# Where the sums stand between the scores: a graph attention kernel with one round behind every second set, its own places in a block's first group, and edges loaded in four parts

## The chip, the cores and the metric

The kernel runs on one core of one Trainium2 chip. The metric is the device time of one execution in microseconds (us); lower is better. Three runs of the kernel before gave 10911.48, 10919.42 and 10927.48 us, median 10919.42.

## What is computed

Four graph layers act on `x` (3327 nodes, 128 features) with one adjacency matrix `adj` (3327 x 3327). Each ends in a residual addition and a layer norm. The change touches only layer 0, an attention in which the edges are added twice to the scores:

```python
q = (x @ Wq.T).reshape(d, n, h)      # d = 128, n = 3327, h = 8
k = (x @ Wk.T).reshape(d, n, h)
v = (x @ Wv.T).reshape(d, n, h)
a = jnp.einsum('dnh,dmh->dnm', q, k) * d ** -0.5
a = a + adj + adj
a = jax.nn.softmax(a, axis=2)
out = jnp.einsum('dnm,dmh->dnh', a, v).reshape(n, h * d) @ Wo.T
x = layernorm(x + out)
```

So there are 128 attention matrices of 3327 x 3327, each with only 8 values to a row of q, k and v: 1.4 thousand million exponentials, for which the scores are a cheap product and the sums another one.

## The kernel before, in words

**Blocks, steps, sets.** The queries are cut into seven chunks of 476 columns (`CW`), the keys into four stretches of 7, 7, 6 and 6 tiles of 128 (`KBS`). A chunk with a stretch is a block; there are 28, half of them seven-tile, half six-tile. In a block the kernel goes through the 128 steps `d`. Within a step the tiles form three sets: of 3, 2 and 2 tiles in a seven-tile block, of 2, 2 and 2 in a six-tile block (`SETS`, L444). Each set has its own region of PSUM, three regions in all (`sc`, L421), and one more bank, `o`, takes the sums.

**Scores.** The edges of a block are loaded into one tile `e_in` (L429 to L441) and, at step 0, turned into PSUM by transposes (L603). They then stay there for all 128 steps. Each step adds the difference of its scores to those of the step before (L610, 64 rows: the query and key halves of this step and, negated, of the step before), so the region always holds edges plus this step's scores. The exponential of a set (L618, on ScalarE) reads the region; the scores of the next step may only be added once it has ended.

**VectorE's share.** In some groups of four steps (`on_vector`, L446) the third set of the first step is not given to ScalarE: `vector_exp` (L568) computes its exponential on VectorE in nine passes, of which only the first (L574) reads PSUM. In a seven-tile block these are the groups g with g mod 4 = 0, 1, 2, in a six-tile block the even g.

**Sums.** Four steps form a group; a block has 32 groups. While the scores of one group are made, the sums of the group before are: `weigh` (L624) multiplies one key tile of the four steps with the padded values, four matmuls of 32 columns each side by side (L635, two instructions each). I call this a round. A group needs seven or six rounds. `PLACES` (L452) says behind which of the twelve sets of the group (place 0 to 11, three to a step) how many rounds stand; a number that occurs twice means two rounds in a row. The pattern is chosen by the number of tiles of the block that the rounds belong to and by g mod 4. After every third group (and the last) the sums in `o` are added to `acc` by VectorE (`flush`, L642 to L650); the first round of the next group starts `o` anew and has to wait for that.

**Order.** TensorE, ScalarE, GpSimd and VectorE run in the order in which the loop at L670 to L682 records their instructions. `prepare` (L546), at the first step of each group, issues on the SP queue the queries and keys two groups ahead (`load_heads`, L456; 1.25 MB in a seven-tile block: `kt` and `qt`, three buffers each) and the values one group ahead. GpSimd then copies the values into a padded tile (L515). VectorE copies the queries of the next group within its partitions (L499 to L501), asked for at step 0 of a group with a VectorE set and at step 1 of the others. VectorE's passes wait in a list and are recorded in small portions by a running account of costs (`clock`, L585).

**Background.** Beside the attention the kernel transposes `adj` in 91 pieces of 512 x 256, one per eight groups (`PACE`). `background` (L526), at groups n with n mod 8 = 0, stores the piece that is done (sixteen DMAs on the GpSimd queue, L234) and loads the next one (L184; a piece at the edge of the matrix first has a memset on GpSimd, L176 or L178). `background_work` transposes it on VectorE at n mod 8 = 3 and takes its sums at 7. `ai`, `at` and `e_in` have one buffer each. The edges of the next block are asked for at step 0, behind the last set (L621): two DMAs on the SP queue, of 1344 KB and the rest.

**After the attention** come the output product and layers 1 to 3, from about 10150 us on, with TensorE as the busiest engine.

Of the kernel before, what the change touches and what calls it, by code (L numbers as in the profile page):

```python
# [10 lines left out]
F32 = mybir.dt.float32  # L11
# [8 lines left out]
P = 128  # L20
GROUP = 4
# [3 lines left out]
PACE = 8  # L25
CW = 476
# [24 lines left out]
def kernel(ctx: ExitStack, tc: tile.TileContext, x, adj, wq, wk, wv, wo,  # L51
# [14 lines left out]
    nc = tc.nc  # L66
    N, D = x.shape
# [26 lines left out]
    def flat_ap(dram, at, pattern):  # L94

        f = dram.rearrange("r c -> (r c)")
        if isinstance(at, int):
            base = f[at:at + 1]
        else:
            base = f[ds(at, 1)]  # L100
        return bass.AP(base.tensor, base.offset, pattern)
# [143 lines left out]
    with tc.tile_pool(name="pw", bufs=1) as pw, tc.tile_pool(name="pa", bufs=2) as pa, \  # L245
# [12 lines left out]
        for u in range(NU):  # L258
# [4 lines left out]
            for a, n in ([(0, P)] if full == P else [(0, 112), (112, full - 112)]):  # L263
                nc.sync.dma_start(out=xr[a:a + n, 0:R, :],
                                  in_=flat_ap(x, (base + R * a) * D, [[R * D, n], [1, R * D]]))
            if rest:
                nc.sync.dma_start(out=xr[full:full + 1, 0:rest, :],
                                  in_=flat_ap(x, (base + R * full) * D, [[D, 1], [1, rest * D]]))
# [87 lines left out]
        d = 0  # L356
# [52 lines left out]
    def attention():  # L409
        with tc.tile_pool(name="acc", bufs=1) as accp, tc.tile_pool(name="kq", bufs=3) as kq, \  # L410
# [12 lines left out]
            subs = [(j, min(P, CW - j)) for j in range(0, CW, P)]  # L423
# [2 lines left out]
            groups = [(b, g) for b in range(len(blocks)) for g in range(NHG)]  # L426
            steps = [(b, d) for b in range(len(blocks)) for d in range(D)]

            def load_edges(b):  # L429
                c0, kb = blocks[b]  # L430
                k0, nt = KBS[kb]
                w = min(nt * P, N - k0 * P)
                e = ed.tile([P, len(subs), 7 * P], F32, name="e_in")
                if w < nt * P:
                    nc.gpsimd.memset(e[:, :, w:nt * P], 0.0)
                nf = CW // P
                nc.sync.dma_start(out=e[:, 0:nf, 0:w],
                                  in_=flat_ap(adj, c0 * N + k0 * P, [[N, P], [P * N, nf], [1, w]]))
                nc.sync.dma_start(out=e[0:CW - nf * P, nf, 0:w],
                                  in_=flat_ap(adj, c0 * N + (nf * P * N + k0 * P), [[N, CW - nf * P], [1, w]]))  # L440
                return e  # L441


            SETS = {7: [(0, 3), (3, 2), (5, 2)], 6: [(0, 2), (2, 2), (4, 2)]}  # L444

            def on_vector(nt, g):  # L446

                return g % 4 != 3 if nt == 7 else g % 2 == 0

            PLACES = {7: ((0, 0, 4, 7, 7, 10, 10), (0, 0, 4, 7, 7, 9, 10), (1, 1, 4, 6, 8, 10, 10),  # L452
                          (0, 2, 3, 5, 7, 8, 10)),
                      6: ((0, 0, 3, 6, 8, 10), (0, 2, 4, 5, 7, 9)) * 2}

            def load_heads(b, g):  # L456

# [66 lines left out]
            loaded, worked, turning = [], [], []  # L524

            def background(n):  # L526
                if n % PACE == 0 and worked:
                    piece_store(pe, *worked.pop(0))
                if n % PACE == 0 and pieces:
                    u, c = pieces.pop(0)  # L530
                    loaded.append((u, c, piece_load(pe, u, c)))

            def background_work(n):
                if n % PACE == 3 and loaded:
                    u, c, ai = loaded.pop(0)
                    steps = piece_work(pe, u, c, ai)
                    worked.append((u, c, next(steps)))
                    next(steps)
                    clock[1] += 2.4
                    turning.append(steps)  # L540
                if n % PACE == 7 and turning:
                    clock[1] += 2.4
                    for _ in turning.pop():
                        pass
# [49 lines left out]
            def exponents(b, d, si):  # L594
                kb = blocks[b][1]
                nt = KBS[kb][1]
                t0, n = SETS[nt][si]
                s = sc[si]
                if d == 0:
                    for i in range(n):  # L600
                        tl = tile_at(nt, t0 + i)[2]
                        for j, (q0, w) in enumerate(subs):
                            nc.tensor.matmul(s[:, i, q0:q0 + w], lhsT=edges[b][0:w, j, tl * P:(tl + 1) * P],  # L603
                                             rhs=ident[0:w, 0:w], is_transpose=True,
                                             start=(j == 0), stop=True, skip_group_check=True)
                kt, qt = heads[b, d // GROUP]
                k = d % GROUP
                for i in range(n):
                    rg, pos, _ = tile_at(nt, t0 + i)
                    nc.tensor.matmul(s[:, i, 0:CW], lhsT=kt[64 * rg:64 * rg + 64, k, pos * P:(pos + 1) * P],  # L610
                                     rhs=qt[64 * rg:64 * rg + 64, k, :],
                                     start=False, stop=True, skip_group_check=True)
                e = ex.tile([P, (3, 2, 2)[si], CW], F32, tag=f"e{si}", name=f"e{si}", bufs=(6, 7, 8)[si])
                if on_vector(nt, d // GROUP) and (d % GROUP, si) == (0, 2):
                    vector_exp(e[:, 0:n, :], s[:, 0:n, 0:CW], (b, d // GROUP))
                    clock[1] += 1.2
                else:
                    nc.scalar.activation(e[:, 0:n, :], s[:, 0:n, 0:CW], AF.Exp, scale=2.0)  # L618
                for i in range(n):
                    es[b, d, t0 + i] = e[:, i, :]  # L620
                if d == 0 and si == len(SETS[nt]) - 1 and b + 1 < len(blocks):  # L621
                    edges[b + 1] = load_edges(b + 1)

            def weigh(b, g, r):  # L624

# [35 lines left out]
            queue, place = [], 0  # L661
            with tc.manual_schedule(engines={mybir.EngineType.PE, mybir.EngineType.Activation,
                                             mybir.EngineType.Pool, mybir.EngineType.DVE}):
                edges[0] = load_edges(0)
                for n in range(2):
                    heads[groups[n]] = load_heads(*groups[n])
                for _, _, step in copy_queries(*groups[0]):
                    step()
                values[groups[0]] = load_values(*groups[0])
                for b, d in steps:  # L670
                    prepare(b, d)
                    for si in range(len(SETS[KBS[blocks[b][1]][1]])):
                        vector_work(b)
                        exponents(b, d, si)
                        for _ in range(PLACES[len(queue_of)][d // GROUP % 4].count(place) if queue else 0):
                            weigh(*queue.pop(0))
                        place += 1
                    if d % GROUP == GROUP - 1:
                        while queue:
                            weigh(*queue.pop(0))  # L680
                        queue_of = [(b, d // GROUP, r) for r in range(KBS[blocks[b][1]][1])]
                        queue, place = list(queue_of), 0  # L682
                while queue:
                    weigh(*queue.pop(0))
                while stores:
                    store(*stores.pop(0))
# [558 lines left out]
```

## Time and profile before

| | |
|---|---|
| median of three runs | 10919.42 us |
| the profiled execution's own time | 10915.5 us |
| its span, first to last instruction | 10913.7 us |
| granted TensorE clock, mean | 0.995 |
| TensorE matmuls, weight loads busy | 97%, 38% of the span |
| ScalarE busy | 90% |
| VectorE busy | 77% |
| GpSimd busy | 15% |
| first exponential starts, last one ends | 334.9, 10141.6 us |
| ScalarE busy in the first and second seven-tile block shown below | 362.43 and 362.32 us |
| the six-tile blocks after them | 319.66 and 319.87 us |

How to read it: a group line names line, engine, operation, tiles, shapes and count, then busy time and mean duration, then the idle time of the engine just before these instructions and what ended it. A timeline line names start, duration, engine, line, operation and count of merged instructions, with the idle time before the first in brackets. "PEld" is TensorE's loading of weights, "SPq" the queue in which SyncE issues DMAs. Matmuls are pipelined and their ends are modelled, so 97% does not say that TensorE has nothing to give. The stretches of four blocks, 1739.8 to 3137.4 us, with busy time and count of each engine, the clock and the share of the DMA engines:

```profile
1739.80:2110.00 370.20, 363.27 (x2712) 128.56 (x2708) 326.48 (x344) 362.43 (x360) 68.86 (x108) 1.00 0.86 129
2110.00:2479.30 369.30, 363.00 (x2715) 128.46 (x2711) 325.97 (x344) 362.32 (x361) 60.75 (x98) 1.00 0.84 126
2479.30:2808.00 328.70, 320.76 (x2340) 106.83 (x2336) 251.35 (x276) 319.66 (x369) 58.00 (x103) 1.00 0.83 129
2808.00:3137.40 329.40, 321.10 (x2337) 107.12 (x2333) 250.33 (x272) 319.87 (x370) 74.07 (x132) 1.00 0.86 135
```

The columns after the stretch are its length, then TensorE's matmuls, its weight loads, VectorE, ScalarE and GpSimd.

### The profile page before, as it was taken

How to read it: one execution, taken by the hardware profiler on the slowest of the kernel's cores; microseconds unless marked ns; L12 is line 12 of the kernel's file. 1: busy time of each engine (PE TensorE's matmuls, PEld its weight loads, DVE VectorE, ACT ScalarE, POOL GpSimd, SP SyncE). 2: the span in 40 equal slices, each digit the busy share in tenths (PEclk: the TensorE clock that was granted, in tenths of full speed). 3: DMA queues.
4: the chain of work that ended last, by engine and by line, in shares of the span. 5: the costliest groups of instructions: out<-in, count | busy, mean ns of one | idle time of the engine just before them, and what ended most of it. 6: DMA issues, size and time to landing. Idle time of an engine off the chain costs nothing. (4 is left out here: it accounts for less than half of the span.)

```text
span 10913.7 us, 202710 instructions
## 1 busy us (share of the span) xinstructions
PE 10590.0 (97%) x76941; PEld 4114.5 (38%) x76941; DVE 8351.7 (77%) x9359; ACT 9774.0 (90%) x10671; POOL 1667.9 (15%) x2742
## 2 busy tenths in 40 slices
PE   8899999999999999999999999999999999999999
PEld 5333333333333333333333333333333333333779
DVE  6788778887788877788877888778887788777312
ACT  3799999999999999999999999999999999999400
POOL 0111122111221111211112111121111100001200
PEclk9899999999999999999999999999999999999999
DMA  7888888888888888888888888888888888788676
GB/s 252 155 127 123 129 133 133 128 124 127 136 133 128 124 127 131 136 123 127 131 131 135 115 122 121 123 133 129 126 129 123 120 119 117 116 111 118 209 283 245
DMA packets 995063, 1516.19 MB, mean 139 GB/s; under 512 B 202471, under 2 KB 812577, under 8 KB 980267
## 3 DMA queue, kind: packets, MB, share of 16 engines
q1 hardware_dynamic: 896854, 1371.75, 77.5%
q0 software_dynamic: 79616, 116.88, 4.7%
q8 instruction: 623, 10.21, 0.5%
q10 hardware_dynamic: 17620, 14.49, 0.4%
q14 instruction: 350, 2.87, 0.1%
HBM read 1371.86 MB, written 130.35 MB: 138 GB/s over the span
## 5 line engine op out<-in xcount | busy, mean ns | idle before, releaser
L618 ACT ACTIVATE e<-sc 128x952 f32<-128x952 f32 (+1 forms) x10192 | 9551.3, 1076 | 281.1 <-PE sc L610 274.7
L635 PE MATMUL o<-e,v_pad 128*32 128x476 f32 (+1 forms) x46592 | 5657.5, 573 | 47.1 <-DVE acc L648 39.8
L610 PE MATMUL sc<-qt,kt 64*128 64x476 f32 x23296 | 4503.2, 439 | 178.4 <-ACT e L618 113.1
L610 PEld LDWEIGHTS sc<-qt,kt 64*128 64x128 f32 x23296 | 2197.0, 184 | 4570.9 <-ACT e L618 4015.0
L580 DVE SCALAR_TENSOR_TENSOR e<-e,ey 128x952 f32<-128x952 f32 x1680 | 1932.7, 1150 | 52.3
L515 POOL COPY v_pad<-vs 128x192 f32<-128x192 f32 (+1 forms) x896 | 534.4, 622 | 7986.1 <-DMA vs<-v_img 5559.1
L635 PEld LDWEIGHTS o<-e,v_pad 128*32 128x32 f32 (+1 forms) x46592 | 1027.9, 108 | 1904.7 <-issue 1858.7
L574 DVE TENSOR_SCALAR ey<-sc 128x952 f32<-128x952 f32 x560 | 643.9, 1150 | 1047.2 <-PE sc L610 1041.2
L501 DVE CAST qt<-qt 64x1904 fp32r<-64x1904 f32 x896 | 1032.8, 1153 | 30.4
L499 DVE TENSOR_SCALAR qt<-qt 32x1428 fp32r<-32x1428 f32 x896 | 807.6, 901 | 159.2 <-DMA qt<-q_s 100.6
L234 POOL DMA_DIRECT2D adjT_s<-at x1352 | 785.3, 587 | 234.5 <-DMA adjT_s<-at 162.2
L580 DVE SCALAR_TENSOR_TENSOR e<-e,et 128x952 f32<-128x952 f32 x560 | 647.5, 1156 | 17.8
L576 DVE SCALAR_TENSOR_TENSOR ey<-et,ey 128x952 f32<-128x952 f32 x560 | 645.1, 1152 | 19.4
L580 DVE SCALAR_TENSOR_TENSOR e<-ey 128x952 f32<-128x952 f32 x560 | 642.0, 1146 | 0.0
L1081 PE MATMUL bank<-y,eT 128*128 128x128 f32 (+1 forms) x4056 | 473.9, 276 | 0.4 <-DVE h L1203 0.4
L1081 PEld LDWEIGHTS bank<-y,eT 128*128 128x128 f32 (+1 forms) x4056 | 465.3, 192 | 5.7 <-DVE h L1203 0.6
L648 DVE TENSOR_TENSOR acc<-o,acc 128x476 f32<-128x476 f32 x231 | 150.3, 651 | 312.4 <-PE o L635 312.0
L575 DVE TENSOR_SCALAR et<-ey 128x952 f32<-128x952 f32 x560 | 372.6, 665 | 18.7
L577 DVE TENSOR_SCALAR et<-et 128x952 int32<-128x952 int32 x560 | 371.1, 663 | 19.3
L500 DVE TENSOR_SCALAR qt<-qt 32x476 fp32r<-32x476 f32 x896 | 360.2, 402 | 7.8 <-DMA qt<-lead_s 3.5
L1041 ACT ACTIVATE rstd<-mv,eps 128x1 f32<-128x1 f32 x104 | 30.4, 293 | 265.5 <-DVE mv L1039 265.5
L655 POOL DMA_DIRECT2D o_s<-acc x308 | 191.4, 625 | 34.9 <-DVE acc L648 22.0
(152 smaller groups left out, 2402.6 us busy)
## 6 DMA issues: line engine op xcount, KB each, us to landing
kt<-k_s SPq DMA_DIRECT2D x5320, 96.0 KB
kt<-k_s SPq DMA_DIRECT2D x1764, 128.0 KB
eT<-adjT_s SPq DMA_DIRECT2D x78, 1664.0 KB
qt<-q_s SPq DMA_DIRECT2D x896, 119.0 KB
qt<-q_s SPq DMA_DIRECT2D x1792, 59.5 KB
vs<-v_img SPq DMA_DIRECT2D x224, 224.0 KB
adjT_s<-at POOLq DMA_DIRECT2D x1352, 32.0 KB, 6.0
vs<-v_img SPq DMA_DIRECT2D x224, 192.0 KB
```

What stands on the lines that cost most here:

```text
L234: nc.gpsimd.dma_start(out=flat_ap(adjT_s, (t * P + 32 * q) * NP + c * PIECE, [[NP, 32], [P, ns], [1, P]]), in_=at[32 * i:32 * i + 32].rear ...
L499: return [(0.9, None, lambda: nc.vector.tensor_scalar(qt[32:64, 1:], qf[0:32, 0:GROUP - 1], -1.0, None, ALU.mult)), (0.4, None, lambda: nc ...
L501: (1.2, None, lambda: nc.vector.tensor_copy(qt[64:128], qf[0:64]))]
L515: nc.gpsimd.tensor_copy(vp[:, 32:32 + nt * GROUP * 32].rearrange("p (x c) -> p x c", c=32)[:, :, 0:H], vs.rearrange("p (x c) -> p x c", c=H))
L574: nc.vector.tensor_scalar(y, x, -58 * math.log(2.0), 2 / math.log(2.0), ALU.max, ALU.mult)
L575: vec.append((0.7, of, lambda: nc.vector.tensor_scalar(t, y, ROUND, None, ALU.add)))
L576: vec.append((1.2, of, lambda: nc.vector.scalar_tensor_tensor(y, t, ROUND, y, ALU.subtract, ALU.subtract)))
L580: vec.append((1.2, of, lambda i=i, a=a: nc.vector.scalar_tensor_tensor(e, e if i else y, a, t if i == len(POLY) - 1 else y, ALU.add, ALU.m ...
L610: nc.tensor.matmul(s[:, i, 0:CW], lhsT=kt[64 * rg:64 * rg + 64, k, pos * P:(pos + 1) * P], rhs=qt[64 * rg:64 * rg + 64, k, :], start=False ...
L618: nc.scalar.activation(e[:, 0:n, :], s[:, 0:n, 0:CW], AF.Exp, scale=2.0)
L635: nc.tensor.matmul(o[32 * j:32 * j + 32, 0:CW], lhsT=values[b, g][:m, c:c + 32], rhs=es[b, g * GROUP + j, r][:m, :], start=(r == 0 and u = ...
L1081: nc.tensor.matmul(ps[:n, 0:D], lhsT=e[:m, s, :n], rhs=y[:m, s, col:col + D], start=(s == 0), stop=(s == T - 1))
```

## The change

Five things are altered, none of which adds or removes arithmetic:

1. **The groups with a VectorE set move by one.** In seven-tile blocks they are now g mod 4 = 1, 2, 3, in six-tile blocks the odd g. The first group of every block is therefore one in which ScalarE computes all twelve sets.
2. **New places.** The six rounds of six-tile blocks stand behind places 0, 2, 4, 6, 8 and 10 in every group. Seven-tile blocks get four new patterns.
3. **Own places in the first group of a block** (`FIRST`): no round before place 4, then mostly two in a row. As before, the pattern is chosen by the number of tiles of the block that the rounds belong to, which in a first group is the block before.
4. **Edges in four parts.** `load_edges(b, j)` loads one of the four row stretches (128, 128, 128 and 92 rows) in a DMA of its own, behind the last set of steps 0, 8, 16 and 24.
5. **Background.** Stores and loads at n mod 8 = 2 instead of 0, transposes at 4 instead of 3, sums at 0 instead of 7.

```diff
-            def load_edges(b):
+            def load_edges(b, j):
...
-                e = ed.tile([P, len(subs), 7 * P], F32, name="e_in")
-                if w < nt * P:
-                    nc.gpsimd.memset(e[:, :, w:nt * P], 0.0)
-                nf = CW // P
-                nc.sync.dma_start(out=e[:, 0:nf, 0:w],
-                                  in_=flat_ap(adj, c0 * N + k0 * P, [[N, P], [P * N, nf], [1, w]]))
-                nc.sync.dma_start(out=e[0:CW - nf * P, nf, 0:w],
-                                  in_=flat_ap(adj, c0 * N + (nf * P * N + k0 * P), [[N, CW - nf * P], [1, w]]))
-                return e
+                if j == 0:
+                    edges[b] = ed.tile([P, len(subs), 7 * P], F32, name="e_in")
+                    if w < nt * P:
+                        nc.gpsimd.memset(edges[b][:, :, w:nt * P], 0.0)
+                q0, n = subs[j]
+                nc.sync.dma_start(out=edges[b][0:n, j, 0:w],
+                                  in_=flat_ap(adj, (c0 + q0) * N + k0 * P, [[N, n], [1, w]]))
...
-                return g % 4 != 3 if nt == 7 else g % 2 == 0
+                return g % 4 != 0 if nt == 7 else g % 2 == 1
...
-            PLACES = {7: ((0, 0, 4, 7, 7, 10, 10), (0, 0, 4, 7, 7, 9, 10), (1, 1, 4, 6, 8, 10, 10),
-                          (0, 2, 3, 5, 7, 8, 10)),
-                      6: ((0, 0, 3, 6, 8, 10), (0, 2, 4, 5, 7, 9)) * 2}
+            PLACES = {7: ((0, 2, 4, 4, 7, 7, 9), (0, 0, 3, 7, 7, 10, 10), (0, 0, 3, 6, 6, 9, 9), (0, 0, 3, 6, 7, 10, 10)),
+                      6: ((0, 2, 4, 6, 8, 10),) * 4}
+
+            FIRST = {7: (4, 4, 5, 7, 7, 10, 10), 6: (4, 4, 7, 7, 10, 10)}
...
             def background(n):
-                if n % PACE == 0 and worked:
+                if n % PACE == 2 and worked:
                     piece_store(pe, *worked.pop(0))
-                if n % PACE == 0 and pieces:
+                if n % PACE == 2 and pieces:
...
             def background_work(n):
-                if n % PACE == 3 and loaded:
+                if n % PACE == 4 and loaded:
...
-                if n % PACE == 7 and turning:
+                if n % PACE == 0 and turning:
...
-                if d == 0 and si == len(SETS[nt]) - 1 and b + 1 < len(blocks):
-                    edges[b + 1] = load_edges(b + 1)
+                if d % (2 * GROUP) == 0 and d // (2 * GROUP) < len(subs) and si == len(SETS[nt]) - 1 \
+                        and b + 1 < len(blocks):
+                    load_edges(b + 1, d // (2 * GROUP))
...
-                edges[0] = load_edges(0)
+                for j in range(len(subs)):
+                    load_edges(0, j)
...
-                        for _ in range(PLACES[len(queue_of)][d // GROUP % 4].count(place) if queue else 0):
-                            weigh(*queue.pop(0))
+                        if queue:
+                            at = PLACES[len(queue_of)][d // GROUP % 4] if d >= GROUP else FIRST[len(queue_of)]
+                            for _ in range(at.count(place)):
+                                weigh(*queue.pop(0))
```

## The prediction

> **What bounds the kernel now.** I read the page, then the table of waits, then ScalarE's timeline alone, then the timeline of all engines at three spots.
>
> ```profile
> L618 ACT ACTIVATE e<-sc 128x952 f32<-128x952 f32 (+1 forms) x10192 | 9551.3, 1076 | 281.1 <-PE sc L610 274.7
> L635 PE MATMUL o<-e,v_pad 128*32 128x476 f32 (+1 forms) x46592 | 5657.5, 573 | 47.1 <-DVE acc L648 39.8
> L610 PE MATMUL sc<-qt,kt 64*128 64x476 f32 x23296 | 4503.2, 439 | 178.4 <-ACT e L618 113.1
> ```
> ```profile
> PEld sc L610 <- ACT e L618: 4015.0, 6332, 1.5
> ACT e L618 <- PE sc L610: 274.7, 585, 25.8
> ```
>
> The exponentials (L618) take 9551 us of the 9807 us between the first (334.9) and the end of the last (10141.6). TensorE and ScalarE wait for each other: three PSUM sets rotate, so a set's scores (L610) wait until its exp of the step before has ended. What can be won is ScalarE's idle time, so I look at where it stands idle. In a six-tile block's start:
>
> ```profile
> 2474.41 5.84 ACT L618 ACTIVATE e<-sc 128x952 f32<-128x952 f32 x6
> 2482.32 0.97 ACT L618 ACTIVATE e<-sc 128x952 f32<-128x952 f32 x1 [2.07 <-PE sc L610]
> 2483.97 4.39 ACT L618 ACTIVATE e<-sc 128x952 f32<-128x952 f32 x5 [0.69 <-PE sc L610]
> 2488.53 4.41 ACT L618 ACTIVATE e<-sc 128x952 f32<-128x952 f32 x5 [0.17 <-PE sc L610]
> ```
>
> Five exps in 4.39 us, the first 0.97: ends lie (4.39-0.97)/4 = 0.856 us apart. In the same way three-tile sets cost 1.254. So ScalarE's floor of a group is, for six tiles, 12 x 0.856 = 10.27 us (9.42 when VectorE takes one set), for seven tiles 11.86 (11.01). I assigned the L618 records in order to block, step and set; medians per group, from end to end: six tiles 9.93 (VectorE group) and 10.29 (other); seven tiles 11.11, 11.37, 11.33 and 11.87 (g mod 4 = 0 to 3). First and second group of a block: 12.76 and 10.79, 13.85 and 11.79. Over the floor, a block loses 14 us (six) or 11 (seven). A VectorE group of a six-tile block:
>
> ```profile
> 2643.51 0.66 PE L610 MATMUL sc<-qt,kt 64*128 64x476 f32 x2 [0.34 <-DMA vs<-v_img]
> 2644.10 1.80 PE L635 MATMUL o<-e,v_pad 128*32 128x476 f32 x16
> 2645.83 0.92 PE L610 MATMUL sc<-qt,kt 64*128 64x476 f32 x6
> 2646.36 4.47 ACT L618 ACTIVATE e<-sc 128x952 f32<-128x952 f32 x5 [0.33 <-PE sc L610]
> 2646.65 1.15 DVE L574 TENSOR_SCALAR ey<-sc 128x952 f32<-128x952 f32 x1 [0.29 <-PE sc L610]
> ```
>
> Two rounds stand between the scores of places 0 and 1, and ScalarE idles. Prices: two rounds hold TensorE 1.73 us until the next scores, one 0.93 (timeline, 2646.68 to 2647.62); scores to exp 0.53; scores to the next round 0.41, 0.58 after a wait. Last, a hold-up of the SP queue:
>
> ```profile
> 6048.74 0.97 POOL L176 MEMSET ai<- 128x1024 f32 x1
> 6049.74 0.79 SPq L184 DMA_DIRECT2D ai<-in_adj_dram  x2
> 6050.97 1.02 SPq L469 DMA_DIRECT2D qt<-q_s  x3
> 6062.69 0.89 DVE L499 TENSOR_SCALAR qt<-qt 32x1428 fp32r<-32x1428 f32 x1 [8.34 <-DMA qt<-q_s]
> 6065.63 2.21 ACT L618 ACTIVATE e<-sc 128x952 f32<-128x952 f32 x2 [8.28 <-PE sc L610]
> ```
>
> **What the Trainium skill says.** "Perfetto Trace Analysis", section "DVE / Act Engine Instruction": a record runs from ALU start to write acknowledge, and the next may prefetch before that. The trace agrees: exps last 0.97 or more but end 0.856 apart, so an exp can start some 0.10 before the last one's end. "ScalarE: Activation LUTs", section "Step-by-step": 0.833 ns per element. An estimate from it, 952 x 0.833 = 0.793 us and 1428 x 0.833 = 1.190, is 0.063 under both measured spacings: no exp gets cheaper. "DMA: Bandwidth & Descriptors", section "Queues, rings and completion order": each engine consumes one ring's descriptors in ring order, so a load issued by SP behind the edges waits for their bytes; the next lines show it.
>
> **The change part by part.** Work is the same: equally many exps, rounds, scores and passes on VectorE. Only positions change. Sum against the profiled execution's own 10915.5 us (span 10913.7), 3.9 under the median.
>
> *1. Six tiles, one round behind every second set.* In the group without VectorE the rounds at 4 and 5 were adjacent; that cost 0.02 over the floor and goes. In the VectorE group let place 9's exp end at 0; saturated, ends follow at 0.86 (10), 1.71 (11), 2.57 (0), 3.42 (1). Before: scores 0 at 0.05, two rounds from 0.64, scores 1 at 2.37, exp at 2.90, while ScalarE could start at 2.57-0.10 = 2.46: 0.44 lost (records: 1.298-0.856 = 0.44), and 0.07 behind it. After: round at 0.51, scores 1 at 1.44, scores 2 wait for place 11 (1.76), round at 2.23, scores 3 at 3.16, exp at 3.69. Place 2 is VectorE's, so ScalarE is through with place 1 and could start at 3.32: 0.37 lost, 0.45 if the hand-over takes the waited price. So the stall moves from place 1 to place 3. Gain per pair of groups 0.52+0.02-0.41 = 0.12; x15 x14 blocks = 25 us. Ends: 0.1 lost (gain 90), or 0.65 (22 worse). The accumulator's flush (L648, 0.65, then the round at place 0): 5 x 0.36 us a block before, now about 1.6 in ten places: 3 us gained.
>
> *2. First group.* Twelve (eight) transposes L603 take 1.38 (0.97) to the scores (timeline, 2107.83 to 2109.21 and 2477.70 to 2478.67). Before, two rounds stood at place 0 too. Now none until 4, and ScalarE has all twelve sets. Six tiles: exp 1 comes 0.48 late, exp 2 0.53, exp 8 0.43 to 0.67 (two rounds at 7): with place 5's round behind a seven-tile block, 1.45 or 2.17 over the floor; the second group, VectorE's now, 1.0 with the flush. Sum 2.8 against 3.34+0.52 = 3.86: 1.05 x 14 = 15 us. Seven tiles: 0.66 or 1.44, then 0.65, so 1.7 against 2.84+0.78 = 3.62; from this 0.3 goes for the third group, now under part 3's 0.34: 1.6 x 14 = 22. The last group of a block is now VectorE's and TensorE has less in hand at its end: the first transposes come 0.1 later, 2 us lost.
>
> *3. Seven tiles.* Same chain by hand. First VectorE group (0,0,3,7,7,10,10): 0.08 behind the double round at 0, 0.08 at place 4 because of the round at 3. Second: its (0,0) follows (10,10), as in the old second: 0.34; then 0.15 at place 7, where L574 (behind the copies L499 to L501) holds the scores of 5. Third 0.15, plain group 0. Sum 0.80 per four groups against 0.10+0.36+0.33 = 0.79: nothing. Ends 0.45 and 1.2: 38 gained or 46 lost over 112 fours. A flush in the second VectorE group holds VectorE's queue, behind it the third's L574, for which the scores of place 5 wait: about 0.46 x 3 a block, 1.1 net x 14 = 15 lost.
>
> *4. Edges in four parts.* The 1.7 MB behind step 0 was issued in one go, beside a piece of 0.5 MB and 1.25 MB of heads, at 130 GB/s. The third group then waits for queries (L499 waits 1.97 at 3166.2, 4.19 at 367.4): groups too long by 6.0, 1.3, 1.3, 1.3 and 0.8. Now 0.46 MB in each of four groups, the piece moved to the third. Each issue costs SP under 0.5 us, and the heads queued behind have eleven us of slack. Parts 1 to 3 wait for nothing new. Gain 11; ends 0 and 14.
>
> *5. Background two groups later.* The SP queue at 6049.7 waited for the memset behind POOL's stores, and the queries behind it came late: that group took 21.07 instead of 11.24. It recurs in group 12, but without a VectorE set and with the copies first asked for a step later; I take 3 us of stall: gain 7, ends 0 and 10. Stores (about 13 us of POOL) and loads keep two groups of cover; if that is gone, a wait of that order per piece.
>
> Sum: 25+3+15+22-2+0-15+11+7 = 66 us: 10849.5 for the profiled execution, 10853 for the median.
>
> **Rivals.** *A, more slack than my chain has*: TensorE runs ahead in the plain group, and the skip costs 0.1; seven tiles reach 0.45. For it: the plain groups lie at the floor. Against: TensorE can't be further ahead than the set rotation allows. With all of both 66+65+38 = 169, with half of both 117: about 10800. *B, the stall only moves*: the double round that goes is paid back in full at the skip, so part 1's 25 fall away and part 2's 35 halve, while 4 and 5 give 18 and flushes cost 12: 23 gained, 10896. For it: 0.37 and 0.44 are close. Against: the L499 waits go in any case. *C, slower*: VectorE's first pass in the seven-tile blocks. Rounds moved from 4 to 3 ask for scores 5 some 0.7 us earlier, and VectorE is busy 326 of 370 us there. If L574 ends over 2.7 us after place 1's exp began (I have 2.2), each second and third VectorE group loses 0.5: 16 x 14 x 0.5 = 112, less 66: 10965.
>
> **How the numbers follow.** About 0.2% (22 us) is what a measurement tells from no change. Forecast 0.56, A 0.20, B 0.12, C 0.12 (A reaches from 10800 on down to 10750). The range reaches to A's inner part and stops before C: 10770 to 10930. Faster: forecast and A, 0.75; same: B and a rest, 0.13; slower: 0.12.
>
> **What would show it.** Six-tile VectorE groups at 9.8 to 9.9 us with the idle time at place 3 and none at place 1; first groups near 11.9 (six) and 12.9 (seven), without double rounds before place 4; no wait of L499 in third groups; the 8 us idle stretch gone or below 4. Wrong if six-tile VectorE groups fall to 9.5 (A), or L610 waits for L574 much longer than the 162.9 us of now (C).

## The result and the profile after

| | before | after |
|---|---|---|
| median of four runs, us | 10923.45 (10911.48 to 10932.62) | 10855.78 (10851.08 to 10858.90) |
| ratio of the runs, 95% interval | | 0.9938 (0.9921 to 0.9956) |
| the profiled execution's own time, us | 10915.5 | 10858.9 |
| from the first exponential's start to the last one's end, us | 9806.7 | 9748.8 |

The kernel is 0.6% faster, as forecast (10853). The two profiled executions lie 56.6 us apart; the forecast, made against that execution, had 66. By these two the sum was some 9 us too large. A fourth run of the kernel before, slower than the other three, moved its median up by 4; the later runs of the same kernel, with medians of 10914.88 to 10920.15, put the difference at 59 to 64 us. The time is saved in the attention: 57.9 us between the first and last exponential.

The groups of the page after and three waits of its table (L635 of before is L636 now, the other lines keep their numbers):

```profile
L618 ACT ACTIVATE e<-sc 128x952 f32<-128x952 f32 (+1 forms) x10192 | 9544.9, 1111 | 228.4 <-PE sc L610 197.2
L636 PE MATMUL o<-e,v_pad 128*32 128x476 f32 (+1 forms) x46592 | 5623.6, 573 | 13.8 <-DVE acc L649 7.4
L610 PE MATMUL sc<-qt,kt 64*128 64x476 f32 x23296 | 4519.8, 442 | 161.2 <-ACT e L618 69.1
```
```profile
PEld sc L610 <- ACT e L618: 3895.0, 6382, 1.4
ACT e L618 <- PE sc L610: 197.2, 543, 4.5
PEld sc L610 <- DVE ey L574: 134.5, 168, 2.5
```

The counts are the same, and ScalarE's busy time nearly is (9551.3 before); what fell is its idle time, 281.1 to 228.4. Of this, 25.8 us before and 24.4 after stand ahead of the very first exponential, when the attention has not begun; the profile puts the 24.4 down to a load, so that they are not in the 197.2. Within the attention the waits for scores fell from 248.9 to 197.2 us, and the longest of them from 8.28 (shown in the prediction) to 4.55. Read the mean of one exponential with care: it grew from 1076 to 1111 ns, though no exponential became slower. A record starts before the one ahead of it has ended, and the longer ScalarE goes without an idle stretch, the earlier the starts creep; from end to end it is 0.856 us in both traces.

In a six-tile VectorE group (all engines, then ScalarE alone over two pairs of groups):

```profile
2643.89 0.70 PE L610 MATMUL sc<-qt,kt 64*128 64x476 f32 x4
2644.52 1.00 PE L636 MATMUL o<-e,v_pad 128*32 128x476 f32 x8
...
2645.45 0.81 PE L610 MATMUL sc<-qt,kt 64*128 64x476 f32 x4
...
2646.03 2.68 ACT L618 ACTIVATE e<-sc 128x952 f32<-128x952 f32 x3 [0.30 <-PE sc L610]
```
```profile
2625.93 19.81 ACT L618 ACTIVATE e<-sc 128x952 f32<-128x952 f32 x23 [0.30 <-PE sc L610]
2646.03 19.81 ACT L618 ACTIVATE e<-sc 128x952 f32<-128x952 f32 x23 [0.30 <-PE sc L610]
```

The four scores at 2643.89 are places 1 and 2. The round behind them holds TensorE until the scores of place 3 start at 2645.45, and the exponential of place 3 starts 0.58 us later, after an idle stretch. There is now one such stretch in 23 exponentials; before, there was one ahead of place 1 and a small one in the plain group. The first group of a six-tile block, ScalarE alone:

```profile
2470.09 0.96 ACT L618 ACTIVATE e<-sc 128x952 f32<-128x952 f32 x1 [0.33 <-PE sc L610]
2471.38 0.97 ACT L618 ACTIVATE e<-sc 128x952 f32<-128x952 f32 x1 [0.33 <-PE sc L610]
2472.77 3.54 ACT L618 ACTIVATE e<-sc 128x952 f32<-128x952 f32 x4 [0.42 <-PE sc L610]
2476.75 1.82 ACT L618 ACTIVATE e<-sc 128x952 f32<-128x952 f32 x2 [0.45 <-PE sc L610]
2479.05 5.42 ACT L618 ACTIVATE e<-sc 128x952 f32<-128x952 f32 x6 [0.48 <-PE sc L610]
```

Idle stretches of 0.3 to 0.5 us ahead of places 0, 1, 2, 6 and 8 have taken the place of 2.07 and 0.69 ahead of places 1 and 3. The one at place 0 is new: the block's first exponential itself now waits. A second VectorE group of a seven-tile block:

```profile
1938.79 1.15 DVE L501 CAST qt<-qt 64x1904 fp32r<-64x1904 f32 x1
...
1939.96 1.15 DVE L574 TENSOR_SCALAR ey<-sc 128x952 f32<-128x952 f32 x1
...
1941.17 0.91 PE L610 MATMUL sc<-qt,kt 64*128 64x476 f32 x5 [0.32 <-DVE ey L574]
...
1942.01 1.80 PE L636 MATMUL o<-e,v_pad 128*32 128x476 f32 x16
...
1944.27 0.96 ACT L618 ACTIVATE e<-sc 128x952 f32<-128x952 f32 x1 [0.20 <-PE sc L610]
```

VectorE's copies (L499 to L501) hold its first pass L574, this holds the scores of place 5, two rounds follow, and place 7 is late.

For the balance I took each trace's L618 records in order, assigned them to block, group and set, and subtracted ScalarE's floor (0.856 us for each two-tile and 1.254 for each three-tile exponential). A group lasts from the end of the last exponential ahead of it to the end of its own last one. Sums over the 14 blocks of a kind, in us over the floor:

| | before | after | gained | forecast |
|---|---|---|---|---|
| six tiles, groups 2 to 30 | 133.6 | 88.9 | 44.7 | 28 |
| six tiles, groups 0 and 1 | 53.9 | 40.7 | 13.2 | 15 |
| seven tiles, groups 0 and 1 | 61.8 | 35.4 | 26.4 | 27 |
| seven tiles, groups 2 to 30 | 113.4 | 127.7 | -14.3 | -2 |
| last groups of both | 6.4 | 18.6 | -12.2 | -2 |
| sum | | | 57.8 | 66 |

Two entries of the last column do not quite match their rows. The 2 us in the row of the last groups were forecast for later first transposes, and the balance counts that wait in group 0. And the seven-tile row holds 15 us of forecast flush losses, of which 5 belong to group 31, a last group.

### The profile page after: what moved, and what is told of

It is laid out like the page before. It is cut to its first block, busy times and chain, and to the rows that moved or that the text cites. A ratio compares the mean times of both kernels' runs of the same rounds, so it can differ in the third digit from the quotient of the medians.

```text
span 10857.1 us, 202867 instructions
## 1 busy us (share of the span) xinstructions
PE 10588.6 (98%) x76941; PEld 4138.6 (38%) x76941; DVE 8398.4 (77%) x9359; ACT 9767.3 (90%) x10671; POOL 1991.4 (18%) x2742
## 5 line engine op out<-in xcount | busy, mean ns | idle before, releaser
L618 ACT ACTIVATE e<-sc 128x952 f32<-128x952 f32 (+1 forms) x10192 | 9544.9, 1111 | 228.4 <-PE sc L610 197.2
L636 PE MATMUL o<-e,v_pad 128*32 128x476 f32 (+1 forms) x46592 | 5623.6, 573 | 13.8 <-DVE acc L649 7.4
L610 PE MATMUL sc<-qt,kt 64*128 64x476 f32 x23296 | 4519.8, 442 | 161.2 <-ACT e L618 69.1
L610 PEld LDWEIGHTS sc<-qt,kt 64*128 64x128 f32 x23296 | 2205.1, 184 | 4509.5 <-ACT e L618 3895.0
L515 POOL COPY v_pad<-vs 128x192 f32<-128x192 f32 (+1 forms) x896 | 729.6, 840 | 7600.5 <-DMA vs<-v_img 5944.1
L636 PEld LDWEIGHTS o<-e,v_pad 128*32 128x32 f32 (+1 forms) x46592 | 1043.3, 108 | 1903.9 <-issue 1870.7
L574 DVE TENSOR_SCALAR ey<-sc 128x952 f32<-128x952 f32 x560 | 643.9, 1150 | 824.3 <-PE sc L610 803.2
L501 DVE CAST qt<-qt 64x1904 fp32r<-64x1904 f32 x896 | 1038.1, 1159 | 30.6
L499 DVE TENSOR_SCALAR qt<-qt 32x1428 fp32r<-32x1428 f32 x896 | 816.3, 911 | 121.3 <-DMA qt<-q_s 80.8
L234 POOL DMA_DIRECT2D adjT_s<-at x1352 | 848.7, 634 | 228.3 <-DMA adjT_s<-at 173.9
L576 DVE SCALAR_TENSOR_TENSOR ey<-et,ey 128x952 f32<-128x952 f32 x560 | 645.0, 1152 | 19.4
L500 DVE TENSOR_SCALAR qt<-qt 32x476 fp32r<-32x476 f32 x896 | 380.1, 424 | 18.5 <-DMA qt<-lead_s 12.2
L656 POOL DMA_DIRECT2D o_s<-acc x308 | 256.6, 837 | 30.8 <-DVE acc L649 20.2
```

The costliest lines, as they stand in the source:

```text
L234: nc.gpsimd.dma_start(out=flat_ap(adjT_s, (t * P + 32 * q) * NP + c * PIECE, [[NP, 32], [P, ns], [1, P]]), in_=at[32 * i:32 * i + 32].rear ...
L499: return [(0.9, None, lambda: nc.vector.tensor_scalar(qt[32:64, 1:], qf[0:32, 0:GROUP - 1], -1.0, None, ALU.mult)), (0.4, None, lambda: nc ...
L500: (0.4, None, lambda: nc.vector.tensor_scalar(qt[32:64, 0], before, -1.0, None, ALU.mult)),
L501: (1.2, None, lambda: nc.vector.tensor_copy(qt[64:128], qf[0:64]))]
L515: nc.gpsimd.tensor_copy(vp[:, 32:32 + nt * GROUP * 32].rearrange("p (x c) -> p x c", c=32)[:, :, 0:H], vs.rearrange("p (x c) -> p x c", c=H))
L574: nc.vector.tensor_scalar(y, x, -58 * math.log(2.0), 2 / math.log(2.0), ALU.max, ALU.mult)
```

## The experiments

The experiments fall into three batches (1, 3, 4 and 5; 6 to 9; 2, 10 and 11). The kernels of a batch share a chip with runs of the kernel before, whose median was 10915.6, 10920.15 and 10914.88. The changed kernel was not run again in them, and the kernel before differs by 5 us between batches, so a difference of a few microseconds from the changed kernel's 10855.78 counts only where the traces show it too.

**1. The edges in one go again.** Behind step 0, as two DMAs:

```diff
-                q0, n = subs[j]
-                nc.sync.dma_start(out=edges[b][0:n, j, 0:w], ...
+                nf = CW // P
+                nc.sync.dma_start(out=edges[b][:, 0:nf, 0:w], ...
+                nc.sync.dma_start(out=edges[b][0:CW - nf * P, nf, 0:w], ...
...
-                if d % (2 * GROUP) == 0 and d // (2 * GROUP) < len(subs) and si == len(SETS[nt]) - 1 \
+                if d == 0 and si == len(SETS[nt]) - 1 \
```

> The changed kernel, with the edges of the next block again loaded in one go behind step 0. Theory (the burst of 1.7 MB makes the queries of the third group late): third groups of some seven-tile blocks become too long again by 1 to 6 us, 5 to 11 us in all, so about 10861 to 10867; less than in the kernel before is possible, because the piece of the adjacency is now loaded two groups later and no longer falls into the same burst. Rival (the waits of the kernel before came from the piece and not from the edges): third groups stay as they are, 10856.

Measured 10855.95 (10855.08 to 10857.22), ratio 0.9945 (0.9928 to 0.9962): no difference in the time. In ScalarE's timeline the long wait of block 0 is back (17.93 us for the third group), and the third group of block 20 is long again (12.91), where the median of third groups is 11.59:

```profile
373.54 2.22 ACT L620 ACTIVATE e<-sc 128x952 f32<-128x952 f32 x2 [3.74 <-PE sc L612]
```

(L620 is the exponential here.) These two cost 7.6 us over the median. The profiled execution of the changed kernel has 5.6 us in six-tile blocks that this one has not, of which more below; so the two traces come out nearly alike. Why the other runs agree is not shown, since they left no trace. So the edges do make third groups late, but in the changed kernel in only two blocks; that the piece no longer falls into the same group is the likely reason, which no run tests alone.

**2. The edges in four parts alone**, on the kernel before (`load_edges` itself as in the change).

```diff
-                edges[0] = load_edges(0)
+                for j in range(len(subs)):
+                    load_edges(0, j)
...
-                if d == 0 and si == len(SETS[nt]) - 1 and b + 1 < len(blocks):
-                    edges[b + 1] = load_edges(b + 1)
+                if d % (2 * GROUP) == 0 and d // (2 * GROUP) < len(subs) and si == len(SETS[nt]) - 1 \
+                        and b + 1 < len(blocks):
+                    load_edges(b + 1, d // (2 * GROUP))
```

> The kernel before, with nothing altered but the edges in four parts. Theory (the burst is what makes the queries of third groups late): the third groups of blocks 0, 8, 16 and 20 lose their 6.0 and three times 1.3 us, 10 us less, 10908. Rival (the piece loaded in the same group is enough for part of the waits): third groups keep 1 us or more in some blocks, 10911 to 10917.

Measured 10906.8 (10902.68 to 10911.42), 8 us under the kernel before; the ratio is 0.9992 (0.9984 to 1.0001), so the time alone doesn't prove it. The trace does: no third group of a block is more than 0.5 us over the median, and seven-tile groups 2 to 30 come to 104.2 us over the floor instead of 113.4. The theory holds.

**3. No places of their own for first groups.**

```diff
-    at = PLACES[len(queue_of)][d // GROUP % 4] if d >= GROUP else FIRST[len(queue_of)]
+    at = PLACES[len(queue_of)][d // GROUP % 4]
```

> The changed kernel, but a block's first group takes the ordinary places of its number instead of its own. Theory: rounds behind places 0 and 2 stand between the transposes again. By the chain of ends, place 1's exp comes 1.4 us late (six tiles) or 1.1 us (seven), place 3's 0.5 to 0.7, against 0.5 and 0 with own places; the later double rounds fall away in part. First groups become longer by about 1.0 to 1.6 us, 28 to 40 us in all: 10884 to 10896. Rival (the gain of the first group came only from giving ScalarE all twelve sets): no change, 10856.

Measured 10871.56 (10868.85 to 10874.1), ratio 0.9960 (0.9946 to 0.9974), 16 us over the changed kernel and less than expected. ScalarE at the same spot:

```profile
2471.69 0.96 ACT L618 ACTIVATE e<-sc 128x952 f32<-128x952 f32 x1 [0.32 <-PE sc L610]
2473.93 0.96 ACT L618 ACTIVATE e<-sc 128x952 f32<-128x952 f32 x1 [1.28 <-PE sc L610]
2475.32 0.96 ACT L618 ACTIVATE e<-sc 128x952 f32<-128x952 f32 x1 [0.42 <-PE sc L610]
```

First groups lose 88.7 us over the floor instead of 55.3, so 33 more, as the chain gave. But second groups lose 10.5 instead of 20.8: with `FIRST` the rounds that were put off leave TensorE late, and the second group pays 10 us of it back. I had not counted that here. The split of the first two groups' gain follows: 39.6 us in the balance, of which `FIRST` is 23 and the rest of the change, with ScalarE doing all twelve sets of a first group, 16.5. The rival, that `FIRST` gives nothing, is refuted.

**4. The six-tile places alone**, on the kernel before.

```diff
-    6: ((0, 0, 3, 6, 8, 10), (0, 2, 4, 5, 7, 9)) * 2}
+    6: ((0, 2, 4, 6, 8, 10),) * 4}
```

> The kernel before, with nothing altered but the places of six-tile blocks: one round behind places 0, 2, 4, 6, 8 and 10. Theory (places alone set the six-tile gain): VectorE groups 9.83 us with the idle time ahead of place 3 instead of place 1, the others 10.28 also after a flush, 45 us less, and some 5 us more from the first groups: 10870 to 10876. Rival (the gain needs the VectorE groups to have moved by one, which also moved the background passes and the flushes): 10900 or more.

Measured 10874.64 (10867.65 to 10884.58), ratio 0.9964 (0.9949 to 0.9978), 41 us under the kernel before. Groups of 9.83 and 10.28 us, and 92.5 us over the floor in groups 2 to 30, against 133.6. The places alone carry the six-tile gain; moving the VectorE groups isn't needed for it.

**5. The old seven-tile patterns**, turned by one group with the VectorE groups.

```diff
-    PLACES = {7: ((0, 2, 4, 4, 7, 7, 9), (0, 0, 3, 7, 7, 10, 10), (0, 0, 3, 6, 6, 9, 9), (0, 0, 3, 6, 7, 10, 10)),
+    PLACES = {7: ((0, 2, 3, 5, 7, 8, 10), (0, 0, 4, 7, 7, 10, 10), (0, 0, 4, 7, 7, 9, 10), (1, 1, 4, 6, 8, 10, 10)),
```

> The changed kernel, with the seven-tile patterns of the kernel before, turned by one group so that each VectorE group keeps its old pattern. Theory (the new seven-tile patterns gave nothing: four groups lose 0.92 us over ScalarE's floor, the old ones lost 0.79): 0.13 us less in each of some 100 fours, about 10 to 15 us less, 10841 to 10846. Rival (the old patterns were only good beside the old background and flush positions): the same or up to 20 us more.

Measured 10833.27 (10828.32 to 10833.53), ratio 0.9923 (0.9906 to 0.9940): 22 us less than the changed kernel. In the traces 17.6 us of this lie in the seven-tile groups 2 to 30 (2.0 of them in one held-up group of block 16), and 5.1 in six-tile groups, whose places are the same: there the changed kernel's profiled execution has waits that part 5 below explains. So the new seven-tile patterns are a loss of some 16 us inside a change that wins. A second VectorE group here, VectorE's first pass, the rounds and ScalarE:

```profile
1935.90 6.89 ACT L618 ACTIVATE e<-sc 128x952 f32<-128x952 f32 x7 [0.25 <-PE sc L610]
...
1937.01 1.15 DVE L574 TENSOR_SCALAR ey<-sc 128x952 f32<-128x952 f32 x1
1937.32 1.01 PE L636 MATMUL o<-e,v_pad 128*32 128x476 f32 x8
...
1938.26 1.24 PE L610 MATMUL sc<-qt,kt 64*128 64x476 f32 x7
...
1939.43 1.80 PE L636 MATMUL o<-e,v_pad 128*32 128x476 f32 x16
```

L574 comes as late as in the changed kernel, 2.8 us into the group in both. But the round stands behind place 4, so the scores of place 5 come after it and need not wait, and the double round stands at 7 and not at 6: no idle stretch after place 1. The group takes 11.39 us against 11.66.

**6. VectorE's copies behind its first pass.**

```diff
-                if d % GROUP == 1 - on_vector(KBS[blocks[b][1]][1], d // GROUP) and n + 1 < len(groups):
+                if d % GROUP == 1 and not on_vector(KBS[blocks[b][1]][1], d // GROUP) and n + 1 < len(groups):
...
+                while vec:
+                    vec.pop(0)[2]()
                 nc.vector.tensor_scalar(y, x, -58 * math.log(2.0), 2 / math.log(2.0), ALU.max, ALU.mult)
+                n = of[0] * NHG + of[1]
+                if n + 1 < len(groups):
+                    vec.extend(copy_queries(*groups[n + 1]))
```

> The changed kernel, but in groups with a VectorE set the three query copies (L499 to L501) are recorded behind VectorE's first pass (L574) of that group and no longer ahead of it. Same work. Theory (in the second VectorE group of seven-tile blocks the copies hold L574, L574 holds the scores of place 5, and the double round at 6 then makes place 7 late by 0.33 us): L574 starts as soon as its scores are there, the idle time ahead of place 7 shrinks from 0.33 to 0.1 or less, second VectorE groups 11.67 to about 11.4 us, 20 to 25 us less in all: 10831 to 10837. Rival (the double round at 6 is too early by itself): places stay late, 10850 to 10856.

Measured 10971.42 (10961.94 to 10979.66), ratio 1.0049 (1.0033 to 1.0066): slower than the kernel before. The second VectorE group did what the theory says, 11.66 to 11.44 us. But the copies' 2.4 us now stand between the passes, which end later, and the third VectorE group's first pass (L576 here, passes L585, exponentials L623) waits for the last of them:

```profile
1972.23 1.15 DVE L585 SCALAR_TENSOR_TENSOR e<-e,et 128x952 f32<-128x952 f32 x1
1973.30 1.14 DVE L576 TENSOR_SCALAR ey<-sc 128x952 f32<-128x952 f32 x1
...
1974.49 0.91 PE L615 MATMUL sc<-qt,kt 64*128 64x476 f32 x5 [1.94 <-DVE ey L576]
1975.02 3.08 ACT L623 ACTIVATE e<-sc 128x952 f32<-128x952 f32 x3 [1.45 <-PE sc L615]
```

Third VectorE groups take 11.65 us instead of 11.15, those with a flush ahead 12.8 or more. That is the mechanism of rival C: with three VectorE groups in a row, what is moved away from one is met by the next.

A second effect lies on top. The trace also records the clock that TensorE is granted, and it is 1.00 nearly everywhere in the attention. In 19 of the 42 third VectorE groups with a flush ahead it is 0.5 for 3.41 us or more, beside a wait of TensorE of 1.8 us or more; these take 14.2 us or more, the others 12.8 to 13.8. That is about 33 us, a third of what this trace has lost against the changed kernel's.

**7. The piece's load ahead of the stores.**

```diff
-                if n % PACE == 2 and worked:
-                    piece_store(pe, *worked.pop(0))
                 if n % PACE == 2 and pieces:
                     u, c = pieces.pop(0)
                     loaded.append((u, c, piece_load(pe, u, c)))
+                if n % PACE == 2 and worked:
+                    piece_store(pe, *worked.pop(0))
```

> The changed kernel, with the load of the next piece recorded ahead of the stores of the last one, so that the memset on GpSimd is ahead of the 16 stores in GpSimd's queue. Theory (SP waits for the memset, the memset for the stores, and the queries behind it come late): the 9 us stretch in group 13 of block 16 goes, nothing else: about 10847. Rival (the stretch comes from the DMA engines being busy with the stores, or from the eight small stores of the maxima): it stays, 10856.

Measured 10850.39 (10848.6 to 10853.88), ratio 0.9937 (0.9920 to 0.9953). In the changed kernel the hold-up had simply moved with the piece, to group 13 of block 16; here the memset comes first:

```profile
6039.47 0.98 POOL L176 MEMSET ai<- 128x1024 f32 x1
...
6053.75 0.90 DVE L499 TENSOR_SCALAR qt<-qt 32x1428 fp32r<-32x1428 f32 x1 [6.99 <-DMA qt<-q_s]
...
6058.21 0.73 PE L610 MATMUL sc<-qt,kt 64*128 64x476 f32 x1 [4.24 <-DMA vs<-v_img]
```
```profile
6060.02 1.36 ACT L618 ACTIVATE e<-sc 128x1428 f32<-128x1428 f32 x1 [3.93 <-PE sc L610]
6065.93 0.96 ACT L618 ACTIVATE e<-sc 128x952 f32<-128x952 f32 x1 [4.55 <-PE sc L610]
```
```profile
6018.95 0.95 POOL L176 MEMSET ai<- 128x1024 f32 x1
6019.85 2.42 POOL L234 DMA_DIRECT2D adjT_s<-at  x4
```

(The first two fences are the changed kernel, the third this one.) The stretch of 9.0 us is gone. Six smaller delays of 0.6 to 1.0 us have come in blocks 16 and 17, in groups that load a piece, so the traces differ by 6 us in the seven-tile groups. Theory right, size two thirds by the traces. Of the 9.0 us a part is not the wait itself: from 6056.7 to 6066.9 us the changed kernel's TensorE is granted a clock of 0.50, and the double round at place 0, which also waits 1.87 us for the padded values, takes 3.40 us instead of 1.80. In this experiment the clock stays at 1.00 there.

**8. The first VectorE group's last double round at 9.**

```diff
-    ... (0, 0, 3, 7, 7, 10, 10), (0, 0, 3, 6, 6, 9, 9), ...
+    ... (0, 0, 3, 7, 7, 9, 9), (0, 0, 3, 6, 6, 9, 9), ...
```

> The changed kernel, with (0, 0, 3, 7, 7, 9, 9) instead of (0, 0, 3, 7, 7, 10, 10) in the first VectorE group of seven-tile blocks. Theory (the double round at 0 of the next group costs 0.34 us only because the double round before it stands at 10, with five tiles of scores between; from 9 it is seven tiles and a three-tile exp more): the idle time ahead of place 1 of the second VectorE group falls from 0.34 to about 0.1, 25 us less: 10831. Rival (the debt only moves to place 10 or to place 7): 10850 to 10860.

Measured 10859.45 (10853.29 to 10860.33), ratio 0.9943 (0.9926 to 0.9959): nothing gained. First VectorE groups go from 11.14 to 11.49 us, second from 11.66 to 11.31, third from 11.15 to 11.28. The rival was right: the double round that follows two places behind another one is the debt, and it is paid at place 10 (0.34 us) instead of at the next group's place 1.

**9. The six-tile round at 3 instead of 2**, in VectorE groups.

```diff
-    6: ((0, 2, 4, 6, 8, 10),) * 4}
+    6: ((0, 2, 4, 6, 8, 10), (0, 3, 4, 6, 8, 10)) * 2}
```

> The changed kernel, with the second round of the VectorE groups of six-tile blocks behind place 3 instead of 2. Theory (the chain of ends: a round between the scores makes the next exp late, wherever it stands behind the set that ScalarE skips): the idle time moves from place 3 to place 4 and is about 0.5 us instead of 0.41, groups 9.9 us, some 15 to 20 us more in all: 10870 to 10876. Rival (the 0.41 comes from VectorE's first pass or from place 2's own scores, and a later round avoids it): groups near 9.45, 80 us less.

Measured 10932.05 (10928.13 to 10939.08), ratio 1.0011 (1.0005 to 1.0018): 76 us more than the changed kernel, where 15 to 20 were expected.

```profile
2660.88 0.97 ACT L618 ACTIVATE e<-sc 128x952 f32<-128x952 f32 x1 [0.21 <-PE sc L610]
2662.22 18.95 ACT L618 ACTIVATE e<-sc 128x952 f32<-128x952 f32 x22 [0.38 <-PE sc L610]
```

Two idle stretches, not one: places 4 and 5 come 0.32 and 0.49 us late from end to end, so groups take 10.23 us. The stall did move with the round, from place 3 to 4. But I left the next round at 4, right behind it, and didn't follow the chain one place further. The rival, that a later round avoids the loss, is refuted.

**10. The first group's memset on GpSimd.**

```diff
-                    nc.vector.memset(qf[32:64, 0], 0.0)
+                    nc.gpsimd.memset(qf[32:64, 0], 0.0)
```

> The changed kernel, with one memset (L484, the query rows of the next block's first group) on GpSimd instead of VectorE. Theory (in a block's group 30, and in six-tile blocks in group 31, VectorE's queue is held by this memset, which waits for TensorE to be done with the buffer; behind it come the copies and L574, and the scores of place 5 wait): group 30 of seven-tile blocks 12.28 to about 11.7 us, 8 us less, group 31 of six-tile blocks partly, 0 to 5 less: 10843 to 10848. Rival (the wait only moves to the copies, which need the same rows): 10856.

In the changed kernel VectorE in group 30:

```profile
2074.17 0.46 DVE L484 MEMSET qt<- 32x476 f32 x1 [0.32 <-PE sc L610]
...
2078.25 1.15 DVE L574 TENSOR_SCALAR ey<-sc 128x952 f32<-128x952 f32 x1
```

The group began at 2074.96, so L574 comes 3.29 us into it; with the edit the same group begins at 2073.29 and L574 comes at 2076.30, 3.01 us into it. Measured 10845.56 (10844.1 to 10848.17), ratio 0.9936 (0.9921 to 0.9951), 10 us less. Group 30 of seven-tile blocks takes 11.93 us instead of 12.24, and six-tile group 31 9.84 instead of 10.08 in the median; together that is about 8 us in the traces. Ahead of place 5 of group 30 the loss falls from 0.43 to 0.11 us, so the rival is refuted; the 0.48 ahead of place 7 stays.

**11. What the experiments point to**: old seven-tile patterns, load ahead of the stores, memset on GpSimd, on the changed kernel.

> Three edits together on the changed kernel: the old seven-tile patterns turned by one group, the load ahead of the stores, and the memset of the first group's query rows on GpSimd. If their gains add: 22, 6 and 8 us, 10820; if the memset gives nothing, because the old third pattern has place 2 later anyway, 10827.

Measured 10822.59 (10821.6 to 10824.45), ratio 0.9914 (0.9901 to 0.9928): 33 us under the changed kernel and 92 under the kernel before. The gains nearly add (22, 6 and 10 make 38). But in the traces each of the three single gains holds 3 to 5 us of six-tile waits that only the changed kernel's profiled execution has, so how well they add is known to a few microseconds only. ScalarE's wait for scores within the attention, 197.2 in the changed kernel:

```profile
ACT e L618 <- PE sc L610: 189.6, 566, 2.2
```

## Why the prediction was right, point by point

**The way of finding it held**: with equal work, ScalarE's idle places are the whole account, and where the chain of ends had the right order of events it gives them to a few hundredths of a microsecond.

*Part 1, six tiles.* Forecast: the stall goes from place 1 to place 3 and is 0.41. Measured: 1.268 - 0.856 = 0.41 ahead of place 3, nothing ahead of place 1, groups of 9.83. The step was right; experiment 4 shows that places alone do it, and experiment 9 that the stall moves with the round. (The terms give 0.13 a pair and 27 us, where the sum has 0.12 and 25.) The term for flushes was mis-sized: 1.6 us a block forecast, none seen. Groups with a flush take the same 9.83 and 10.28. That is about 22 us to the good and makes 44.7 of 28. That TensorE, which waits for sets in any case (3895 us in all), has that much time is the likely reason. Against this stand 5.6 us in two groups of blocks 3 and 7, below.

*Part 2, first groups.* Forecast 15 and 27 us (the 27 before a deduction for the third group), measured 13.2 and 26.4. Even single groups fit: six tiles 12.41 and 11.56 from start to start, the chain had 12.44 and 11.72. The prediction measured a group from the end of its first exponential to that of the next group's, so that the wait ahead of a block's first exponential fell to the block before. Counted in its way the first groups gained 16.4 and 30.1, and the later first exponentials lost 7 us, where 2 were forecast: in seven-tile blocks they are 0.78 to 1.05 us late, 0.63 before.

The last groups lose 12 us. In seven-tile blocks it is 5: group 31 loses 0.45, just as groups 7 and 19 do, which also have a flush ahead; part 3 had that. The 7 us in six-tile blocks are a term that the prediction put at nothing. In the last block of each chunk VectorE's copies for the next block's first group stand ahead of L574, and one of them (L500) waits for rows that are loaded last, 2.33 us in block 11. The memset L484 costs most one group earlier, in group 30 of seven-tile blocks, and is counted in part 3.

*Part 3, seven tiles.* Forecast: nothing from the patterns and 15 lost to flushes, 5 to the third group. The places of the stalls were right: 0.34 ahead of place 1 of the second VectorE group, one ahead of its place 7. The latter is 0.31, not 0.15, so four groups lose 0.92 and not 0.80, against 0.81 before. Its cause, the round at 3 with a late L574 and a double round at 6, is shown by experiments 5 and 6. A flush ahead of the third VectorE group costs 0.3, not 0.46. By the medians groups 2 to 30 lose 26 us. Of these, 8 are extra in group 30, where VectorE's queue is held by the memset L484. The prediction did not have that, and experiment 10 wins 6 of them back. The other 18, with the 5 of group 31, stand against a forecast of 20.

*Part 4, edges.* Forecast 11. Experiments 1 and 2 show 7.6 and 9 by the trace: right in mechanism and nearly in size.

*Part 5, background.* Forecast: the hold-up of the SP queue falls from 9.8 us to 3. It did not: 9.0 us. I reasoned that a copy asked for one step later would forgive most of it. But the first scores of the next group start at 6058.21, 2.07 us after the last copy has ended, so they waited for more than the queries. The keys come behind these in the queue and are the likely reason; the profile names the values, whose load is issued right behind them. Then the values were late too and TensorE's clock was halved, as experiment 7 tells. Experiment 7 also shows the order of memset and stores as the cause. And one risk that I had named but priced at nothing came up in the profiled execution: the transposes wait for the stores.

```profile
2926.57 1.25 DVE L199 STREAM_TRANSPOSE at<-ai 128x1024 f32<-128x1024 f32 x1 [5.66 <-DMA adjT_s<-at]
...
2929.62 1.41 PE L636 MATMUL o<-e,v_pad 128*32 128x476 f32 x8 [2.40 <-DVE acc L649]
...
2931.78 0.96 ACT L618 ACTIVATE e<-sc 128x952 f32<-128x952 f32 x1 [2.69 <-PE sc L610]
```

VectorE stood 5.66 us, the flush behind it was late, the round at place 0 waited for it, and ScalarE for that; a stretch of 3.41 us with a clock of 0.5 followed. It cost ScalarE time in two of 91 pieces here, in one in experiments 7 and 8, in none in most others; what decides it stays open. VectorE waits like this, 1.5 us or more ahead of a transpose, in four pieces here and in none of the kernel before. The new positions leave two groups between stores and transposes where there were three; that is the likely reason, but no run moves them alone.

So the forecast total is good partly by luck, because terms offset each other: the six-tile flushes were 22 us too dear, against group 30 with the memset 8, the last six-tile groups 7, the hold-up 6, the stores 6 and the seven-tile terms 3 too cheap.

**The rivals.** A (the skip costs 0.1) is refuted by 0.41 in every VectorE group, B by the six-tile gain. C did not happen: L610 waits for L574 134.5 us, less than the 162.9 of before (200.6 and 187.2 if both of TensorE's rows are added). But its mechanism is in the trace (the wait of L610 for L574 behind the copies), and experiment 6 shows that it is close: moving 2.4 us of copies is enough for 116 us, a part of them by the clock.

## What to carry to other kernels

When two engines hand buffers to each other, list the idle time of the one with the larger floor by its place in the loop, from end to end of its records; a chain of a few ends per place then tells where a reordering moves the stall, and it must be followed until the slack is back, not just to the first stall. Measure each part of a reordering alone: here a change that won 0.6% held one part that lost 0.15 to 0.2%. In an engine that runs in order, look at what stands ahead of the instruction that others wait for: a memset or a copy for later use can hold it as well as its own work does.

## What the runs showed of the hardware that was not expected

The mean duration of an ACTIVATE in the profile is no measure of its cost when the engine is saturated: 1076, 1111 and 1120 ns for the same instructions in the kernel before, the changed one and that of experiment 11, while spacing from end to end stayed at 0.856 us for 952 columns and 1.254 for 1428. Starts creep ahead by about 0.012 us with each exponential of an unbroken stretch and fall back at the next idle one, so start-to-start distances (0.844) look shorter than what the engine keeps up over a long stretch.

A wait of TensorE can cost more than its own length. In experiment 6 TensorE stood for more than 1.5 us 46 times in the attention; beside 22 of these waits the granted clock was 0.5 for 3.41 us or twice that, and as long waits elsewhere left it at 1.00. In the changed kernel a round of eight matmuls took 1.69 us in such a stretch and 1.01 outside. What decides whether the clock falls stays open.
